# Spreading the softmax maxima over the partitions: 32 by 32 turns and a trip through DRAM in place of TensorE transposes and selector products

## The chip, the cores and the metric

The kernel runs on one core of one Trainium2 chip. The core has five engines that work side by side and meet through semaphores: TensorE (PE in the profile, its weight loads PEld) multiplies matrices into PSUM; VectorE (DVE) and ScalarE (ACT) work element by element; GpSimd (POOL) is used here only to start accumulating transfers; SyncE (SP) starts nearly all other transfers. The transfers themselves run on 16 DMA engines.

The metric is the device time of one execution in microseconds (us); lower is better. The kernel before has a median of 2479.35 us over three runs (2477.35 to 2480.38).

## The reference

One transformer block on x of 4 sequences by 1024 tokens by 512 features, all in float32, conditioned on a vector of 128 numbers per sequence. Cut to what matters:

```python
def norm(x, t, gw, gb, bw, bb):          # RMS norm with gain and bias from the condition t
    g = (t @ gw.T + gb)[:, None, :]
    b = (t @ bw.T + bb)[:, None, :]
    return g * x * rsqrt(mean(x * x) + 1e-6) + b

def attention(x, Wq, Wk, Wv, Wo):        # 16 heads of 32 features
    q, k, v = (x @ W.T for W in (Wq, Wk, Wv))
    attn = einsum('blhd,bmhd->bhlm', q, k) / sqrt(32)
    p = softmax(attn, axis=-1)           # exp(attn - max) / sum of exp
    return einsum('bhlm,bmhd->blhd', p, v) @ Wo.T

h = x + attention(norm(x, ...), ...)
h = h + (silu(n @ gate_w.T) * (n @ hid_w.T)) @ out_w.T      # n = norm(h, ...), hidden width 2048
out = x + h
```

The change concerns the softmax: the maximum over all 1024 keys, for each query and head, has to be subtracted from the scores before the exponential, and the exponentials have to be summed over the keys.

## The kernel before

**Tiling.** Scores are held transposed: the 128 partitions are keys, the free axis is queries. So the maximum over keys, and the sum over keys, run across partitions. One *unit* (number `r`) is 256 keys (`k` = 0, 1: two tiles of 128) for a group of 4 heads (`HG`) and 256 queries (`HQ`): a tile `raw[r]` of 128 partitions by 2 x 4 x 256. Four units (`UN`) cover the 1024 keys and make one *softmax group*, `j = r // UN`. There are 64 groups and 256 units.

**The slots.** A hand-written loop (`while g < END`) emits the instructions of one slot per `g`; `kind = g % 4`. PE, DVE, ACT and POOL run their instructions in exactly the order in which the loop emits them; the order on SP's queue is left to the framework's scheduler. In slot `g` the loop emits

- for unit `g`: `scores` (PE, into the 4-bank PSUM tile with tag `sc`, of which there is one), `keep` (ACT copies it to `raw`), `running_max` (DVE, once per key tile, into `rmax[j]`);
- for unit `g - 5`: `shifted` (DVE subtracts the maxima, spread to all partitions in the tile `shift[j]`, from `raw`) and `exponential` (ACT);
- for unit `g - 6`: `weighted` (PE, product with V into `av`) and `accumulate` (POOL starts a 1 MB accumulating transfer that adds `raw` into the group's first `raw` tile).

So the running maximum of group `j` is complete at the end of a slot of kind 3; `max_T` and `parts` turn and reduce it in the following slot of kind 0; and in the slot of kind 1 after that its first unit is shifted.

**From running maximum to `shift` (before).** `max_T`: PE transposes `rmax` in 8 blocks of 128 by 128 into the `sc` PSUM tile. `parts`: DVE takes the maximum of each row, and splits it by four small instructions into three bfloat16 parts (so that their sum is exact in float32). In kind 1, `parts_T`: PE transposes the parts, ACT copies them to `mT`. `spread`: PE multiplies a 0/1 matrix `select` with `mT`, which writes the negated maxima to all partitions, for two heads at a time; ACT copies each half to `shift`. `shifted` runs in two halves in kind 1, one for each half of the heads.

**Sums.** `fold_sum` (DVE, kind 0) adds the two key-tile halves of the accumulated exponentials of group `g // 4 - 3`, `sums` (PE) multiplies them with a matrix of ones, `sums_out` (ACT) takes the result out, `inverse` (DVE reciprocal) and `normalize` follow, as a rule in kind 2.

**The feed-forward part** runs in the same slots from slot 60 (`FS`) on, one hidden block `p` of 128 features per two slots. It multiplies by Strassen-like sums: seven products, each of two 128-row halves, named by their number: `pair_26` and `copy_156` in the even slot, then the *filler* (`contract`, four output-projection products of 512 columns, evicted by `take_contract`), then `pair_7` and `sub_5` at the end of the even slot; `pair_3`, `gate_tanh`, `pair_15` (of block `p + 1`), `take_5`, `add_15`, `gate`, `pair_4`, `hidden` in the odd slot. `pair_4` adds into a bank half that `sub_5` (DVE) has written, so it waits for `sub_5`. Before slot 60 the PE time is filled by *chains* (projections to keys, queries and values): one per slot, and a second one at the end of even slots. After every eighth group four chains of `project_out` come between.

**Queues.** Weight loads (`load_f`: `fa`, `fw`; `load_ow`: `ow`), keys, queries, V and small round trips through DRAM (`compact`, `take`, `put`, `spread_inverse` for the norms) are all issued by SP.

Of the kernel before, what the change touches and what calls it, by code (L numbers as in the profile page):

```python
# [11 lines left out]
BF16 = mybir.dt.bfloat16  # L12
# [12 lines left out]
def tile_cond_transformer_block(  # L25
# [41 lines left out]
    ident_bf = const.tile([P, P], BF16, tag="ident_bf", name="ident_bf")  # L67
    make_identity(nc, ident_bf)
# [6 lines left out]

    NP = 3 * HG
    split = [const.tile([P, QT, P], BF16, tag=f"split{i}", name=f"split{i}") for i in range(2)]
    for t in split:
        nc.vector.memset(t, 0.0)

    pick = const.tile([NP, HG], F32, tag="pick", name="pick")
    nc.vector.tensor_reduce(pick, ident[:NP, :NP].rearrange("p (h i) -> p h i", i=3), AX.X, ALU.add)
    select = const.tile([NP, HG, P], BF16, tag="select", name="select")
    nc.vector.tensor_copy(select, pick.unsqueeze(2).to_broadcast([NP, HG, P]))
# [26 lines left out]
    raw, rmax, shift, mT, av, acc, avs, oT = {}, {}, {}, {}, {}, {}, {}, {}  # L111
# [215 lines left out]
    def max_T(j: int):  # L327
        pt = ps_sc.tile([P, HQ // P, HG, P], F32, tag="sc", name=f"mt{j}")
        for qt in range(HQ // P):
            for i in range(HG):  # L330
                nc.tensor.transpose(pt[:, qt, i, :], rmax[j][:, i, qt * P : (qt + 1) * P], ident)
        state["mt", j] = pt

    def parts(j: int):

        top = sb.tile([P, HQ // P, HG], F32, tag="top", name=f"top{j}")
        nc.vector.tensor_reduce(top, state.pop(("mt", j)), AX.X, ALU.max)
        to = split[j % 2][:, :, :NP].rearrange("p a (h i) -> p a h i", i=3)
        nc.vector.tensor_scalar_mul(to[:, :, :, 0], top, -1.0)
        nc.vector.tensor_tensor(top, top, to[:, :, :, 0], ALU.add)  # L340
        nc.vector.tensor_scalar_mul(to[:, :, :, 1], top, -1.0)
        nc.vector.scalar_tensor_tensor(to[:, :, :, 2], top, -1.0, to[:, :, :, 1], ALU.mult, ALU.subtract)

    def parts_T(j: int):
        pt = ps.tile([P, HQ // P, P], BF16, tag="w", name=f"pt{j}")
        for qt in range(HQ // P):
            nc.tensor.transpose(pt[:, qt, :], split[j % 2][:, qt, :], ident_bf)
# [350 lines left out]
    with tc.manual_schedule(  # L698
# [69 lines left out]
        while g < END:  # L768
# [14 lines left out]
            if kind == 1 and m_on:  # L783
                parts_T(j_m)
# [219 lines left out]
```

## Time and profile before

| quantity | value |
|---|---|
| median of three runs | 2479.35 us |
| the profiled execution | 2480.0 us, of which the span is 2478.1 us |
| granted TensorE clock, mean | 0.998 |
| first slots (chains beside attention) | 86 to 538 us, 31.3 to 32.9 us per group |
| attention beside the feed-forward part | 538 to 2180 us |
| feed-forward part alone | from 2180 us to the end |
| transfers | 501.69 MB |

A group's period can be read from the two `pt` transposes that occur once per group (line 347). From group 18 on they repeat in a pattern of eight: 43.8 us for the group with the four `project_out` chains, 31.6, 32.0, 31.7, 32.4 us for the four with norm work, and three times 30.55 us with neither. I call the last kind a *plain* period.

How to read the lines: a group row gives line, engine, operation, tiles, shapes and count, then busy us and mean ns of one, then the idle time of the engine just before these instructions and what ended it. A timeline row gives start and length in us, then engine, line, operation and count. For matrix products the length includes the pipeline's run-out, so the distance from one start to the next is what counts. A transfer row gives the issuing queue, count, KB each and the median us from issue to landing.

### The profile page before, as it was taken

What the parts mean: (1) busy time and instruction counts of PE and PEld (TensorE: products, weight loads), DVE (VectorE), ACT (ScalarE), POOL (GpSimd) and SP (SyncE); (2) the same over time, 40 slices, a digit from 0 to 9 for tenths busy, and PEclk for the clock granted to TensorE, in tenths of its full rate; (3) what the DMA queues carried; (4) which work ended last, traced back from release to release, by engine and by line L of the source; (5) the groups of instructions that cost most, each with busy time, mean ns of one, the idle gap of its engine ahead of it and who ended that gap; (6) DMA issues with size and microseconds to landing.
All of it is one profiled execution on the core that took longest, in us unless ns stands there. A gap on an engine that the chain in (4) does not pass through costs nothing. (4 is left out here: it accounts for less than half of the span.)

```text
span 2478.1 us, 71138 instructions
## 1 busy us (share of the span) xinstructions
PE 2396.0 (97%) x31785; PEld 1121.8 (45%) x31785; DVE 1943.7 (78%) x2180; ACT 1412.4 (57%) x1495; POOL 172.4 (7%) x207
## 2 busy tenths in 40 slices
PE   8999999999999999999999999999999999999999
PEld 3333333344444444444444444444444444444444
DVE  2688888888789988998899978997899889843332
ACT  3677777766566656665666656665666566512111
POOL 0000000000000000000000000000000000000000
PEclk9999999999999999999999999999999999999999
DMA  6599998989878888888888888788788888853432
GB/s 214 178 299 251 265 259 221 238 201 238 197 193 203 203 218 200 200 211 214 207 197 207 226 191 204 199 226 203 196 201 212 210 197 199 201 159 116 138 134 71
DMA packets 185982, 501.69 MB, mean 202 GB/s; under 512 B 21319, under 2 KB 78663, under 8 KB 158286
## 3 DMA queue, kind: packets, MB, share of 16 engines
q0 software_dynamic: 28656, 208.68, 43.6%
q1 hardware_dynamic: 156734, 288.47, 34.2%
q8 instruction: 250, 4.10, 0.6%
q14 instruction: 54, 0.44, 0.1%
q10 hardware_dynamic: 288, 0.01, 0.0%
HBM read 246.44 MB, written 41.97 MB: 116 GB/s over the span
## 5 line engine op out<-in xcount | busy, mean ns | idle before, releaser
L363 DVE TENSOR_TENSOR raw<-raw,shift 128x2048 f32<-128x2048 f32 (+1 forms) x320 | 593.9, 1859 | 65.2 <-ACT shift L358 62.3
L366 ACT ACTIVATE raw<-raw 128x2048 f32<-128x2048 f32 x256 | 490.8, 1917 | 214.3 <-DVE raw L363 213.8
L317 ACT COPY raw<-sc 128x2048 f32<-128x2048 f32 x256 | 479.6, 1873 | 169.9 <-PE sc L310 129.7
L322 DVE TENSOR_TENSOR rmax<-rmax,raw 128x1024 f32<-128x1024 f32 x384 | 469.5, 1223 | 53.9 <-ACT raw L317 48.2
L106 PE MATMUL pc<-h,ow 128*32 128x512 f32 x4096 | 467.7, 593 | 2.1 <-DMA ow<-in_out_w 1.1
L376 PE MATMUL av<-raw,v 128*32 128x256 f32 x4096 | 274.9, 386 | 50.0 <-ACT raw L366 50.0
L390 POOL DMA_DIRECT2D raw<-raw x192 | 165.3, 861 | 1991.5 <-ACT raw L366 939.1
L310 PE MATMUL sc<-q,k 32*128 32x256 f32 x4096 | 293.3, 400 | 0.2 <-ACT raw L317 0.2
L106 PE MATMUL pa<-x,fa 128*32 128x256 f32 x4096 | 270.0, 381 | 8.8 <-DVE pa L524 8.5
L106 PE MATMUL pa<-sums,fw 128*32 128x256 f32 x4096 | 267.9, 379 | 0.0
L106 PEld LDWEIGHTS pc<-h,ow 128*32 128x32 f32 x4096 | 128.2, 110 | 245.5 <-issue 226.7
L310 PEld LDWEIGHTS sc<-q,k 32*128 32x128 f32 x4096 | 184.9, 184 | 116.5 <-issue 81.5
L106 PE MATMUL pkq<-y,wkq 128*32 128x512 f32 (+1 forms) x1664 | 231.3, 594 | 4.2 <-ACT y L196 4.1
L376 PEld LDWEIGHTS av<-raw,v 128*32 128x32 f32 x4096 | 107.2, 109 | 175.8 <-ACT raw L366 88.0
L106 PEld LDWEIGHTS pa<-x,fa 128*32 128x32 f32 x4096 | 127.6, 110 | 124.7 <-DVE pa L524 30.5
L106 PEld LDWEIGHTS pa<-sums,fw 128*32 128x32 f32 x4096 | 133.2, 110 | 88.2 <-issue 0.5
L539 ACT COPY pb<-pa 128x256 f32<-128x256 f32 x128 | 46.2, 361 | 181.4 <-PE pa L106 180.3
L577 DVE SCALAR_TENSOR_TENSOR res<-pc,res 128x512 f32<-128x512 f32 x128 | 88.2, 689 | 67.2 <-PE pc L106 62.9
L556 ACT ACTIVATE t<-pa 128x512 f32<-128x512 f32 x128 | 78.1, 610 | 109.9 <-PE pa L106 109.5
L106 PE MATMUL pa<-x,fw 128*32 128x256 f32 x2048 | 135.2, 381 | 0.0
L106 PE MATMUL pb<-x,fw 128*32 128x256 f32 x2048 | 134.0, 379 | 1.2 <-ACT pb L539 1.2
L106 PE MATMUL pb<-sums,fa 128*32 128x256 f32 x2048 | 133.9, 379 | 0.0
(106 smaller groups left out, 2152.4 us busy)
## 6 DMA issues: line engine op xcount, KB each, us to landing
raw<-raw POOLq DMA_DIRECT2D x192, 1024.0 KB, 9.1
fw<-sw SPq DMA_DIRECT2D x128, 512.0 KB, 7.0
fa<-in_gh_w SPq DMA_DIRECT2D x128, 384.0 KB, 5.9
ow<-in_out_w SPq DMA_DIRECT2D x128, 256.0 KB, 2.9
wkq<-in_kq_w SPq DMA_DIRECT2D x32, 512.0 KB, 5.9
v<-vs SPq DMA_DIRECT2D x128, 128.0 KB, 5.0
k<-kqs SPq DMA_DIRECT2D x124, 128.0 KB, 7.0
kqs<-st SPq DMA_DIRECT2D x61, 256.0 KB, 7.7
```

The lines of the kernel that those rows point to most:

```text
L106: nc.tensor.matmul(dst[k : k + n, :], w[:, k : k + n], moving, start=start, stop=stop, skip_group_check=seeded)
L310: nc.tensor.matmul(sc[:, i, k, :], keys[rows, k * P : (k + 1) * P], queries[rows, :], start=True, stop=True)
L317: nc.scalar.copy(raw[r].rearrange("p k h q -> p h k q"), state.pop(("sc", r)))
L322: nc.vector.tensor_tensor(rmax[j], rmax[j], raw[r][:, k, :, :], ALU.max)
L363: nc.vector.tensor_tensor(t, t, s.unsqueeze(1).to_broadcast(list(t.shape)), ALU.add)
L366: nc.scalar.activation(raw[r], raw[r], AF.Exp)
L376: nc.tensor.matmul(av[j][i * DH : (i + 1) * DH, :], v[m, u][:, k, i * DH : (i + 1) * DH], raw[r][:, k, i, :], start=(kt == 0), stop=(kt == ...
L390: nc.gpsimd.dma_start(out=acc[j].rearrange("p k h q -> p (k h q)"), in_=raw[r].rearrange("p k h q -> p (k h q)"), accum_op=ALU.add,)
L539: nc.scalar.copy(bank_b[p][:, RIGHT], bank_a[p][:, RIGHT])
L556: nc.scalar.activation(state["t", p], bank_a[p], AF.Tanh, scale=0.5)
L577: nc.vector.scalar_tensor_tensor(r, pp, 0.5, r, ALU.mult, ALU.add)
```

## The change

- `max_T`, `parts`, `parts_T` and the old `spread` go, and with them the bfloat16 identity, `split`, `pick`, `select`, `mT`.
- `max_blocks` (DVE, at the start of kind 0, ahead of `shifted`): `rmax`, 128 by 1024, is turned within blocks of 32 by 32 by two VectorE transposes of 512 columns, and each result is reduced to 16 columns by a maximum; so each partition then holds the maxima over a quarter of the keys.
- `max_T` (PE, kind 0, after the sums): one matrix product with the identity turns the 128 by 32 result to 32 by 128; DVE takes the maximum over the four quarters (`top`, 32 by 32); SP writes it to DRAM (4 KB).
- `spread` (SP): one transfer reads the 1024 maxima from DRAM and writes them to all 128 partitions (`shift`, 512 KB).
- `shifted` subtracts in one instruction in every slot, kind 1 too, where it stands as in the other slots ahead of the slot's other DVE work.
- `fold_sum` goes; `sums` multiplies both halves on PE (8 products instead of 4), and its result and `max_T`'s go to the `sc` PSUM tile (`spare`) instead of a bank of tag `w`.
- `pair_7` and `sub_5` move from the end of the even slot to the odd slot, ahead of `pair_3`.
- `inverse` moves from the end of kind 2 to the end of kind 0.

```diff
-    def max_T(j: int):
-        pt = ps_sc.tile([P, HQ // P, HG, P], F32, tag="sc", name=f"mt{j}")
-        for qt in range(HQ // P):
-            for i in range(HG):
-                nc.tensor.transpose(pt[:, qt, i, :], rmax[j][:, i, qt * P : (qt + 1) * P], ident)
-        state["mt", j] = pt
-    def parts(j: int):
...
-    def parts_T(j: int):
...
-    def spread(j: int, k: int):
...
-    def shifted(r: int, heads: slice = slice(0, HG)):
...
+    CHUNKS = HG * HQ // 32
+
+    def max_blocks(j: int):
+        state["blocks", j] = sb.tile([P, CHUNKS], F32, tag="blocks", name=f"blocks{j}")
+        half = CHUNKS // 2
         for i in range(2):
+            turned = sb.tile([P, half, 32], F32, tag="t", name=f"turned{j}_{i}", bufs=2)
+            nc.vector.transpose(
+                turned.rearrange("p b c -> p (b c)"),
+                rmax[j][:, i * HG // 2 : (i + 1) * HG // 2, :].rearrange("p h q -> p (h q)"),
+            )
+            nc.vector.tensor_reduce(state["blocks", j][:, i * half : (i + 1) * half], turned, AX.X, ALU.max)
+
+    def spare(g: int):
+
+        return ps_sc.tile([P, HG, 2, HQ], F32, tag="sc", name=f"spare{g}")
+
+    def max_T(j: int, banks):
+        pt = banks[:CHUNKS, 1, 0, :P]
+        nc.tensor.matmul(pt, state.pop(("blocks", j)), ident, start=True, stop=True)
+        top = sb.tile([CHUNKS, 32], F32, tag="top", name=f"top{j}")
+        nc.vector.tensor_reduce(top, pt.rearrange("b (a q) -> b q a", a=P // 32), AX.X, ALU.max)
+        state["top", j] = tc.dram_tile([CHUNKS, 32], F32, name=f"tops{j}")
+        nc.sync.dma_start(out=state["top", j], in_=top)
+
+    def spread(j: int):
+
+        shift[j] = sb.tile([P, HG, HQ], F32, tag="shift", name=f"shift{j}")
+        src = state.pop(("top", j)).rearrange("(o b) q -> o (b q)", o=1)
+        nc.sync.dma_start(
+            out=shift[j].rearrange("p h q -> p (h q)"), in_=src.to_broadcast([P, HG * HQ])
+        )
+
+    def shifted(r: int):
+        s = shift[r // UN].unsqueeze(1).to_broadcast(list(raw[r].shape))
+        nc.vector.tensor_tensor(raw[r], raw[r], s, ALU.subtract)
...
-    def fold_sum(j: int):
-        t = acc[j]
-        nc.vector.tensor_tensor(t[:, 0, :, :], t[:, 0, :, :], t[:, 1, :, :], ALU.add)
...
-    def sums(j: int):
-        total = ps.tile([P, HQ], F32, tag="w", name=f"sum{j}")
+    def sums(j: int, banks):
+        total = banks[:, 0, 0, :]
         a = acc.pop(j)
-        for i in range(HG):
-            nc.tensor.matmul(total[i * DH : (i + 1) * DH, :], ones_sum, a[:, 0, i, :], start=True, stop=True)
+        for k in range(2):
+            for i in range(HG):
+                nc.tensor.matmul(
+                    total[i * DH : (i + 1) * DH, :], ones_sum, a[:, k, i, :], start=(k == 0), stop=(k == 1)
+                )
...
-            if kind == 1 and m_on:
-                parts_T(j_m)
             if g < NR:
                 scores(g)
-            if kind == 1 and m_on:
-                spread(j_m, 0)
-            if kind == 0 and n_on:
-                fold_sum(j_n)
+            if kind == 0 and m_on:
+                max_blocks(j_m)
...
-            if x_on and kind != 1:
+            if x_on:
                 shifted(r_x)
...
-            if kind == 1 and m_on:
-                spread(j_m, 2)
-                mT.pop(j_m)
-                shifted(r_x, slice(0, HG // 2))
-                shifted(r_x, slice(HG // 2, HG))
...
+            if kind == 0 and (m_on or n_on):
+                banks = spare(g)
...
                 evict = chain(g, FG)
-                if kind == 0:
-                    take_sums(j_n)
+                if kind == 0 and n_on:
+                    take_sums(j_n, banks)
+                if kind == 0 and m_on:
+                    max_T(j_m, banks)
+                    spread(j_m)
...
-                if kind == 0 and m_on:
-                    columns[0] = P
-                    max_T(j_m)
-                    parts(j_m)
...
                 copy_156(p)
-                if kind == 0:
-                    take_sums(j_n)
+                if kind == 0 and n_on:
+                    take_sums(j_n, banks)
+                if kind == 0 and m_on:
+                    max_T(j_m, banks)
                 if x_on:
                     exponential(r_x)
-                if kind == 0 and m_on:
-                    max_T(j_m)
-                    parts(j_m)
                 one, two, evict = filler(p)
...
                 if evict is not None:
                     evict()
-                pair_7(p)
-                sub_5(p)
+                if kind == 0 and m_on:
+                    spread(j_m)
...
                     evict = chain(g)
+                pair_7(p)
+                sub_5(p)
                 pair_3(p)
...
-            if kind == 0 and n_on and j_n < direct and j_n % GB == GB - 1:
+            if kind == 0 and n_on and j_n < direct:
                 inverse(j_n)
-                normalize(j_n)
+                if j_n % GB == GB - 1:
+                    normalize(j_n)
             if kind == 2 and n_on and j_n < direct and j_n % GB != GB - 1:
 
-                inverse(j_n)
                 if j_n != GB:
                     normalize(j_n)
```

## The prediction

> **What bounds the kernel now.** I read the page's busy line first. TensorE is busy 97% of the span; no other engine comes near, but VectorE has 78%, and the DMA row shows 80 to 90% for as long as attention runs.
>
> ```profile
> PE 2396.0 (97%) x31785; PEld 1121.8 (45%) x31785; DVE 1943.7 (78%) x2180; ACT 1412.4 (57%) x1495; POOL 172.4 (7%) x207
> ...
> DMA  6599998989878888888888888788788888853432
> ```
>
> Then the groups, shapes kept apart, for what the change removes:
>
> ```profile
> L337 DVE TENSOR_REDUCE top<-mt 128x8 f32<-128x1024 f32 x64 | 78.2, 1221 | 4.5 <-PE mt L331 4.5
> ...
> L331 PE MATMUL mt<-ident,rmax 128*128 128x128 f32 x512 | 69.9, 280 | 0.0
> ...
> L357 PE MATMUL sp<-mT,select 12*128 12x256 bf16 x256 | 49.0, 270 | 1.1 <-ACT shift L358 0.7 <-ACT mT L349 0.4
> ```
>
> Then the timeline of one plain period (two `pt` 30.55 us apart), here TensorE alone at its end, in the slot of kind 0:
>
> ```profile
> 1414.45 0.64 PE L408 MATMUL sum<-raw,ones_sum 128*32 128x256 f32 x8
> 1415.02 1.09 PE L331 MATMUL mt<-ident,rmax 128*128 128x128 f32 x8
> 1416.04 3.64 PE L106 MATMUL pc<-h,ow 128*32 128x512 f32 x32
> 1419.50 1.05 PE L106 MATMUL pb<-x,fw 128*32 128x256 f32 x16
> 1420.49 0.27 PE L347 MATMUL pt<-ident_bf,split 128*128 128x128 bf16 x2
> ```
>
> The reader is to see that PE goes from one start to the next without a hole: the way of the maxima costs PE time, but nobody waits for it, because `contract` (3.45 us) and `pair_7` (1.0 us) run while VectorE makes the parts. VectorE itself is busy 27.6 of the 30.5 us, in an order written out by hand.
>
> Last the transfers, and one round trip through DRAM that is there already (the norms'):
>
> ```profile
> raw<-raw POOLq DMA_DIRECT2D x192, 1024.0 KB, 9.1
> fw<-sw SPq DMA_DIRECT2D x128, 512.0 KB, 7.0
> ...
> ow<-in_out_w SPq DMA_DIRECT2D x128, 256.0 KB, 2.9
> wkq<-in_kq_w SPq DMA_DIRECT2D x32, 512.0 KB, 5.9
> ```
>
> ```profile
> 1208.91 0.24 SPq L156 DMA_DIRECT2D sumsf<-totf  x1
> ...
> 1211.73 0.32 SPq L162 DMA_DIRECT2D fewf<-sumsf  x1
> ```
>
> A 2 KB write was followed by its reader 2.8 us later (1.9 us where `invsf` was followed by `totf`). A 512 KB load lands after 5.9 to 7.0 us while attention runs; in the last stretch, with attention over, the same `fw` load needs 3.1 us:
>
> ```profile
> fw<-sw SPq DMA_DIRECT2D x23, 512.0 KB, 3.1
> ```
>
> **What PE saves.** By distances between starts in the plain period: `pt` 0.20, the two `sp` 0.31 and 0.32, `mt` 1.02: 1.85 us per group go. Added: four more sum products, 0.5 us (the eight records of `sum` take 0.57; bounds 0.44, half of a 16-record product at 0.87, and 0.57), and one product with the identity, 0.27 us (bounds 0.13, one `mt` transpose, and 0.31, one `sp`). Net 1.08 us per group, 69 us over 64. Two waits in kind 0 (`weighted` for the exponential 0.3 us, `pair_26` for `add_15` 0.2 us) may go too: 0.5 us per group.
>
> **What ACT and VectorE save.** ACT loses `mT` 0.36 and two copies of 0.59: 1.54 us per group, worth nothing in itself, as ACT is idle 43% of the time; its cover is that idle time. VectorE loses `fold_sum` 1.22 (64 in 78.0 us), the reduction 1.22, four parts 0.71 and 0.2 from halving `shifted` (2.49 against 2.28): 3.35 us. It gains two block turns, two reductions of 512 columns and a small maximum of 128 columns. No turn is in this trace. The nearest rows are 128x512 operations at 0.69; the ends are 0.43 (a 128x256 row, were it twice as fast) and 1.22 (a 128x1024 row, were it half as fast). I take 0.69 and for the small one 0.28 (between 0.17 for 8 columns and 0.43 for 256): 3.04 us, or 2.5 to 4.1. Busy time hardly changes; the place does.
>
> **What it waits for.** Before, `shift` came from PE and ACT within kind 1. Now it needs a write to DRAM, its completion, and a 512 KB read to all partitions, and `shifted` of kind 1 stands in VectorE's order before `sub_5`. Behind a late `shifted` wait `sub_5`, both maxima, `add_15`, `gate` and `hidden`; `pair_4` on PE waits for `sub_5`, and all PE work behind `pair_4` with it. Moving `pair_7` and `sub_5` into the odd slot makes this link: before, `sub_5` stood ahead of `shifted`. On SP, `fa`, `fw`, key and V loads queue behind the two waits (some 2.4 us each period); three `fw` buffers and five key and five V buffers cover that, and without them PE would wait as long.
>
> **The period, walked.** S is the end of the first `shifted` of a group, T the start of the next kind 0 (its `scores`). PE after S: `sub_5` 0.4, `pair_4` 0.98, `scores` 1.08, `weighted` 0.88, `pair_26` 1.73, `contract` 3.43, then kind 3: 1.08 + 0.88 + `pair_7` 0.87 + `pair_3` 0.87 + `pair_15` 1.72 + `pair_4` 0.98. So T = S + 14.9. VectorE's kind 3 ends at T + 1.4, since `add_15` waits for ACT's `take_5` behind the exponential. `max_blocks` 2.6 (starts follow each other 0.07 us faster than durations say) to T + 4.0; `shifted` 2.2 to T + 6.2, `top` to T + 6.5. PE meanwhile: 1.08 + 0.88 + 1.73 + sums 1.0 = T + 4.7, `max_T` to T + 5.0, `contract` to T + 8.4. Write issued T + 6.6, read 2.4 us later (middle of 1.9 and 2.8) at T + 9.0, landing after L, `shifted` 2.4 with its wake-up: next S = T + 11.4 + L. In the gap VectorE has `running_max`, `take_contract` and the reciprocal that was moved there, until T + 11.0. A period is 26.3 + L, where before it is 30.55. **The break-even is L = 4.2 us.**
>
> L is the disputed price. Nearest rows: 5.9 (`wkq`, 512 KB) and 7.0 (`fw`, 512 KB from DRAM scratch), both under traffic; quiet, 3.1. The read meets an accumulating transfer (three per group at 9.1 us fill 27 of 30.5 us) and comes 0.5 us after an `ow` load on its own queue, so it is nearer to the loaded rows: I take 6.4, ends 3.1 and 8.8 (`fw` between 1000 and 1400 us).
>
> Beside this row stands a rule. The Trainium skill, "DMA: Bandwidth & Descriptors", section "Anatomy of one DMA", gives each transfer about 2.0 us fixed plus its bytes at 436 GB/s, mostly the receipt of the write. By it the 512 KB take 3.2 us, as in the quiet rows here, but not the 7.0 us of the loaded ones; the period would be 29.5 us and the kernel faster by some 60 us. The same section says the receipt is longest where the target is DRAM, which speaks against putting the maxima there; 1.9 to 2.8 us here.
>
> **The sum.** After slot 60 there are 50 groups. 44 have no `project_out`: 26.3 + 6.4 - 30.55 = +2.15 us each, +95. Six have four chains of 3.4 us, one of them before `pair_4` of kind 1, which covers the wait: -1.1 each, -7. The first 14 groups have no `pair_4`, only `weighted` of kind 2 behind its exponential: kind 0 takes 1.1 + 0.9 + 3.45 + 1.0 + 0.3; `top` at T + 7.0, read T + 9.5, with 5.8 (`wkq` there) landed 15.3, `shifted` 17.6, exponential 19.6, where PE wanted it at 16.6; then 0.9 + 6.9 + 1.1 + 0.9 + 3.45 gives 32.8 against a mean of 32.3 before: +7. Together +95; the profiled execution's 2480.0 becomes 2575, and as it stands 0.65 us above the median, 2574 to compare with 2479.35. 0.2% (5 us) is what a measurement can tell.
>
> **The rivals.**
> (1) The trip is hidden or short. For it: the quiet 3.1 us, and the reciprocal put into the gap. Against it: DMA at 84% there. At L = 3.1 the plain period is 29.4 (-51), the long ones -7, the first part PE-bound at some 30.1 (-31): 2391. It decides from L below 4.2.
> (2) SP holds the write or the read behind a blocked load: `ow` is seen waiting for the end of `contract`, T + 8.4. A write put behind it is 2.1 us later, 64 times: 2574 + 134 = 2708. For it: SP's order is not written in the kernel. Against it: the loop emits the write first.
> (3) The wait and PE's saving cancel, L between 4.0 and 5.2: 2470 to 2520. For it: a read issued after the accumulate has nearly ended. Against it: all loaded 512 KB rows.
>
> **How the numbers follow.** My case, L from 5.2 to 8.8: 0.56. Rival 1: 0.22, rival 2: 0.10, rival 3: 0.12, of it 0.03 within 0.2%, 0.02 below and 0.07 above. Faster 0.24, same 0.03, slower 0.73. For my case alone the range is 2520 to 2660 (turns at 0.43 or 1.22 move it by -33 or +68). Reaching to rival 1's middle and into rival 2, 2440 to 2680 leaves 0.1 out on either side.
>
> **What would show it.** `shifted` with an idle time ended by the DMA of `shift`, some 4 us per group; PE idle before `pair_4` in kind 1, ended by `sub_5`; landing of `shift` at 6 to 7 us; plain periods of 32 to 33.5 us; `max_blocks` rows at 0.69; the tail after attention unchanged. Wrong if `shift` lands in under 4.2 us, or if a turn costs much more than 0.69.

## The result and the profile after

The changed kernel takes 2912.53 us (median of four runs, 2898.77 to 2919.92) where the kernel before takes 2479.34 us: a ratio of 1.174 with an interval of 1.173 to 1.176. That is 433 us more. The prediction had the sign and the waiting instruction right and the size wrong: it foresaw 95 us more.

The page of the changed kernel, from a run of 2911.5 us (busy line, the rows of PE, its granted clock and the DMA share over the span, the costliest groups, the transfers):

```profile
span 2909.7 us, 71319 instructions
...
PE 2449.3 (84%) x31866; PEld 1157.2 (40%) x31866; DVE 1908.1 (66%) x2048; ACT 1330.1 (46%) x1303; POOL 172.4 (6%) x205
...
PE   8778778888788888887988878887888788889999
...
PEclk9899889999899989998999989999999899999999
DMA  5697788877777777777767767777677777773442
...
L351 DVE TENSOR_TENSOR raw<-raw,shift 128x2048 f32<-128x2048 f32 x256 | 584.9, 2285 | 418.4 <-DMA shift<-tops 418.4
...
L93 PE MATMUL pb<-sums,fa 128*32 128x256 f32 x2048 | 170.0, 459 | 271.4 <-DVE pb L531 271.4
L364 PE MATMUL av<-raw,v 128*32 128x256 f32 x4096 | 304.6, 420 | 101.6 <-ACT raw L354 101.4
...
raw<-raw POOLq DMA_DIRECT2D x192, 1024.0 KB, 9.3
fw<-sw SPq DMA_DIRECT2D x128, 512.0 KB, 7.4
...
shift<-tops SPq DMA_DIRECT2D x64, 512.0 KB, 5.1
```

TensorE falls from 97% to 84% of the span. VectorE's instructions have grown no costlier (1908 us busy against 1944), but 418 us of idle time stand in front of `shifted` (line 351), and the transfer of `shift` ended all of it. The next two rows show how that reaches TensorE: 271 us in front of `pair_4` (`pb<-sums,fa`), ended by VectorE's `sub_5` (line 531), which stands behind `shifted`; and 101 us in front of `weighted`, ended by the exponential, mostly in the first part of the kernel, where there is no `pair_4`. The mean granted clock fell from 0.998 to 0.924, and TensorE's busy time rose by 53 us although the change takes work from it. That second effect is not in the prediction.

The waits of SyncE in the changed kernel (line waited for: us in total, times, longest us):

```profile
SPq L345 <- DMA tops<-top: 282.4, 64, 9.1
SPq L339 <- DVE top L337: 241.2, 46, 6.9
...
SPq L416 <- DMA out<-res: 43.1, 6, 8.8
```

The read (line 345) waits 282 us for the completion of the 4 KB write, 4.4 us each time. The time from one issue to the other is longer: after the first part it is 4.7 us in the mean of 45 groups, and 8.3 us in six others, each the one just ahead of a group with `project_out` chains. Line 416 loads the residual, and its waits come back where those six groups are explained.

One plain period (start, length, engine, line, operation; the idle time before it, and what ended it, in brackets):

```profile
1601.89 0.32 SPq L345 DMA_DIRECT2D shift<-tops  x1
...
1603.05 1.05 PE L93 MATMUL pa<-sums,fw 128*32 128x256 f32 x16
...
1606.78 2.29 DVE L351 TENSOR_TENSOR raw<-raw,shift 128x2048 f32<-128x2048 f32 x1 [5.24 <-DMA shift<-tops]
1608.99 0.42 DVE L531 TENSOR_TENSOR pb<-pb,p 128x256 f32<-128x256 f32 x1
...
1609.47 1.94 PE L93 MATMUL pb<-sums,fa 128*32 128x256 f32 x16 [5.38 <-DVE pb L531]
...
1611.34 2.09 PE L297 MATMUL sc<-q,k 32*128 32x256 f32 x16
...
1626.84 1.15 PE L297 MATMUL sc<-q,k 32*128 32x256 f32 x16
...
1632.06 0.30 PE L335 MATMUL spare<-ident,blocks 128*32 128x128 f32 x1 [0.49 <-ACT total L400]
...
1632.89 0.27 DVE L337 TENSOR_REDUCE top<-spare 32x32 f32<-32x128 f32 x1
1633.19 0.32 SPq L339 DMA_DIRECT2D tops<-top  x1
...
1638.27 0.33 SPq L345 DMA_DIRECT2D shift<-tops  x1
```

This is the prediction's walk, in the measured times of one period. S, the end of `shifted`, is 1609.07, and T, the start of `scores` of the next kind 0, is 1626.84. The write leaves at T + 6.35, the read 5.08 us behind it. At the top of the same list a read at 1601.89 lets `shifted` start 4.89 us later. The sum 17.8 + 6.35 + 5.08 + 4.89 + 2.29 is 36.4 us, and the two reads stand 36.4 us apart. Plain periods differ in their parts: over the twelve groups that were plain before and don't stand just ahead of `project_out` chains, S to T is 17.2 us in the mean, write to read 4.7, and the read's issue to the start of `shifted` 5.5. Look at the lengths of the products too: after the idle time 16 records take 1.94 and 2.09 us, at the next kind 0 the same `scores` take 1.15.

The same kernel in windows around that wait (start and end, us, busy of PE, PEld, DVE, ACT, POOL, then the granted clock, the DMA share and GB/s) shows why:

```profile
1604.00:1608.00 4.00, 0.09 (x4) 0.00 (x0) 1.22 (x1) 0.00 (x0) 0.00 (x0) 1.00 0.97 230
1608.00:1609.40 1.40, 0.00 (x0) 0.00 (x0) 1.40 (x3) 0.29 (x1) 0.00 (x0) 0.67 1.03 233
1609.40:1611.30 1.90, 1.83 (x16) 0.60 (x16) 1.87 (x3) 1.90 (x3) 0.00 (x0) 0.50 1.04 233
...
1613.30:1615.00 1.70, 1.70 (x20) 0.79 (x20) 1.70 (x2) 1.47 (x1) 0.00 (x0) 0.50 1.00 387
1615.00:1617.00 2.00, 2.00 (x40) 1.13 (x36) 1.97 (x3) 0.40 (x1) 0.00 (x0) 0.93 0.20 65
```

TensorE stops at 1604.1. The means of the windows put the fall of the clock to one half at about 1608.5, 4.4 us later, and its return at about 1615.3, 5.8 us after the restart. The Trainium skill, "TensorE: Matmul & The Clock Gate", Part 1, "The HAM clock gate", describes such a gate: the clock halves after at least one idle window of about 3.4 us, and returns after at least one busy window of about 3.4 us. The halving is as the page says; the two times in this example are longer, which "at least one" allows.

Where the 433 us lie can be read from the distances between groups, sorted by the place of the group. "Long" groups have the four `project_out` chains, the "group before" is the one just ahead of them, which has a 1 MB load of the residual on its way. Mean period in us:

```
                      13 first   6 long   6 group before   38 other   sum of the 63
before                  32.24     43.82       30.55          31.52       2063.2
after                   41.49     50.01       43.96          36.51       2490.5
difference, summed      +120      +37         +80            +190        +427
no trip                 32.89     44.50       29.13          29.56       1992.5
previous maxima         34.95     44.72       39.77          31.59       2161.6
busy wait               41.71     49.81       47.27          35.35       2468.1
P7 even                 41.90     47.62       43.84          36.25       2470.8
no accumulate           34.75     44.59       30.45          30.38       2056.5
write from ScalarE      40.09     49.97       40.24          36.66       2455.5
```

(The lower rows are the experiments below.) The tail is as it was: from the turn of the last group's maxima (`pt` before, `max_T` after) to the end are 329 us before and 339 after, and the second holds that group's trip.

### The profile page after: what moved, and what is told of

It is laid out like the page before. It is cut to its first block, busy times and chain, and to the rows that moved or that the text cites. A ratio compares the mean times of both kernels' runs of the same rounds, so it can differ in the third digit from the quotient of the medians.

```text
span 2909.7 us, 71319 instructions
## 1 busy us (share of the span) xinstructions
PE 2449.3 (84%) x31866; PEld 1157.2 (40%) x31866; DVE 1908.1 (66%) x2048; ACT 1330.1 (46%) x1303; POOL 172.4 (6%) x205
## 3 DMA queue, kind: packets, MB, share of 16 engines
q1 hardware_dynamic: 169022, 322.29, 33.5%
## 5 line engine op out<-in xcount | busy, mean ns | idle before, releaser
L351 DVE TENSOR_TENSOR raw<-raw,shift 128x2048 f32<-128x2048 f32 x256 | 584.9, 2285 | 418.4 <-DMA shift<-tops 418.4
L93 PE MATMUL pc<-h,ow 128*32 128x512 f32 x4096 | 477.1, 594 | 0.5 <-DMA ow<-in_out_w 0.5
L93 PE MATMUL pb<-sums,fa 128*32 128x256 f32 x2048 | 170.0, 459 | 271.4 <-DVE pb L531 271.4
L364 PE MATMUL av<-raw,v 128*32 128x256 f32 x4096 | 304.6, 420 | 101.6 <-ACT raw L354 101.4
L297 PE MATMUL sc<-q,k 32*128 32x256 f32 x4096 | 330.5, 442 | 0.1
L297 PEld LDWEIGHTS sc<-q,k 32*128 32x128 f32 x4096 | 206.1, 206 | 205.6 <-issue 127.1
L93 PE MATMUL pkq<-y,wkq 128*32 128x512 f32 (+1 forms) x1976 | 248.0, 623 | 4.1 <-ACT y L183 4.1
L93 PEld LDWEIGHTS pc<-h,ow 128*32 128x32 f32 x4096 | 165.3, 110 | 208.7 <-issue 137.5
L93 PEld LDWEIGHTS pb<-sums,fa 128*32 128x32 f32 x2048 | 69.0, 124 | 346.4 <-DVE pb L531 300.7
L93 PE MATMUL po<-oT,wo 128*32 128x512 f32 x1024 | 127.8, 643 | 14.8 <-DVE h L546 11.7
```

The source lines that it names most:

```text
L93: nc.tensor.matmul(dst[k : k + n, :], w[:, k : k + n], moving, start=start, stop=stop, skip_group_check=seeded)
L297: nc.tensor.matmul(sc[:, i, k, :], keys[rows, k * P : (k + 1) * P], queries[rows, :], start=True, stop=True)
L351: nc.vector.tensor_tensor(raw[r], raw[r], s, ALU.subtract)
L364: nc.tensor.matmul(av[j][i * DH : (i + 1) * DH, :], v[m, u][:, k, i * DH : (i + 1) * DH], raw[r][:, k, i, :], start=(kt == 0), stop=(kt == ...
```

## The experiments

The theory after the result (A): the round trip, write, completion, read to all partitions, stands alone in the path from one group to the next, and it is longer than foreseen because the write completes late while an accumulating transfer of 1 MB is on its way. The rivals: the trip's traffic slows everything else (B); the halved clock makes most of the loss by itself (C); the move of `pair_7` and `sub_5` makes the link (D). The expectations use the letters C and D, with or without a number, for the rival of their own run; outside them, the letters are the ones of this list. Unless a line says otherwise, each time is from one run beside a run of the kernel before on the same chip, which took 2478.5 to 2478.9 us.

**The read takes the previous group's maxima.** The write and the read are both still made, 64 times, but the read no longer waits for this group's write and is issued before it.

```diff
-        src = state.pop(("top", j)).rearrange("(o b) q -> o (b q)", o=1)
+        src = state.pop(("top", j - 1)) if j else state["top", j]
+        src = src.rearrange("(o b) q -> o (b q)", o=1)
...
+                if kind == 0 and m_on:
+                    spread(j_m)
                 if kind == 0 and n_on:
                     take_sums(j_n, banks)
                 if kind == 0 and m_on:
...
-                if kind == 0 and m_on:
-                    spread(j_m)
```

> The changed kernel, but the read that fills shift takes the maxima of the group before, which lie in DRAM long since, and is issued ahead of this group's write. All work and both transfers stay; only the wait for the write's completion goes (softmax does not change with what is subtracted; group 0 alone still reads its own). Theory A (the time is the latency of write and read, standing between the first shifted and pair_4, and the halved TensorE clock after the idle time): read issued at T + 6.3 instead of T + 11.4, first shifted ends at T + 13.8, about when PE comes to pair_4; no long idle, no halved clock; plain periods 29 to 30.5 us, 2380 to 2470 us. Rival B (the added traffic of 34 MB slows everything else): traffic is the same, still above 2800 us. Rival C (the wait counts, the clock does not): 2912 less 64 x 5 us, some 2590 us.

2579.35 us: 333 of the 433 us are gone, with the same bytes on the way. So rival B falls. It is over 100 us more than the expectation gave theory A, and near the 2590 us of the rival that counts the wait and not the clock; but it doesn't speak for that rival, since `shifted` still waits 152 us for `shift` here, and the granted clock is 0.973. The transfers and the wait of this kernel:

```profile
shift<-tops SPq DMA_DIRECT2D x64, 512.0 KB, 7.2
```

```profile
DVE raw L352 <- DMA shift<-tops: 152.0, 55, 9.7
```

Issued earlier, in the middle of an accumulating transfer, the read needs 7.2 us instead of 5.1. What the write's completion cost was thus in part a shift in time: in the changed kernel the read leaves 8.2 us (median) after the last accumulate was started, when that transfer has nearly ended, and here 3.9 us after.

**No trip at all.** Neither write nor read; `shift` is a tile of zeros set once.

```diff
-        state["top", j] = tc.dram_tile([CHUNKS, 32], F32, name=f"tops{j}")
-        nc.sync.dma_start(out=state["top", j], in_=top)
...
+        if "zero" not in state:
+            state["zero"] = sb.tile([P, HG, HQ], F32, tag="shift", name="shift")
+            nc.vector.memset(state["zero"], 0.0)
+        shift[j] = state["zero"]
```

> The changed kernel without the write and the read: shift is one tile of zeros, set once (the turned and reduced maxima are still made, and not used; softmax does not change with what is subtracted, and these scores are far from overflow). It asks what the rest of the change is worth when nobody waits. Theory A: PE saves 1.1 us per group and some waits, less what the moved pair_7 and the sums cost by themselves (29 and 20 us in the kernel before): 2390 to 2450 us, clock 0.998, plain periods about 29 us. Rival C2 (spare bank, moved pair_7 and doubled sums eat the saving): 2470 us and more.

2405.48 us, 73 us below the kernel before; a plain period is 29.0 us. So what TensorE saves is real, and in sum near the 69 us of the prediction; the trip costs 2912.5 - 2405.5 = 507 us. TensorE's 31,866 instructions are busy 2311.2 us here, at a granted clock of 0.996, and 2449.3 us in the changed kernel, at 0.924. The same instructions take 138 us more, and the lower clock is what differs; even counted in full, that is under a third of the 433 us.

**Work in the wait.** To see what the clock costs in time, idle products with the identity keep TensorE busy while it waits: 18 in kind 1 ahead of `pair_4`, where no other chain stands there, and 28 ahead of the first `weighted` of a group before slot 60.

```diff
+    def idle(dst, n: int):
+        for _ in range(n):
+            nc.tensor.matmul(dst, ones_mean, ident, start=True, stop=True)
...
+            if r + UN + 2 < FS:
+                idle(av[j][:, :P], 28)
...
+                if kind == 1 and x_on and not extra:
+                    idle(spare(g)[:, 0, 0, :P], 18)
                 pair_4(p)
```

> The changed kernel, with products that nothing reads put where PE waits: 18 of 128 by 128 by 128 ahead of pair_4 in kind 1 without a chain (about 4.9 us at full clock), 28 ahead of the first weighted product of a group in kind 2 before slot 60. The wait itself stays. Theory A: granted clock stays at 1.0 through the wait, pair_4 and the two stages after it take 0.98, 1.08 and 0.9 instead of 1.9, 2.0 and 1.7 us; 2.5 to 2.9 us less in each of some 50 groups, 2740 to 2800 us. Rival C (the slow products after the wait come from something else, waits for PSUM or transfers): they stay slow and the time stays at 2900 us or rises.

2888.21 us, only 24 us less (the four runs of the changed kernel spread over 21): a miss. The clock rises to 0.970, and behind the wait of a plain period the products run at their full pace (`pair_4` 1.07 us, `scores` 1.15). S to T shrinks there from 17.2 us in the mean to 15.0 in nearly every one, which is the prediction's 14.9. A plain period goes from 36.4 to 34.3. The first part does not move (41.71 against 41.49 us). The group before the long one gets 3.3 us longer, and all of that stands in the trip: from `top` to the start of `shifted` it takes 21.3 us instead of 18.0. The idle products do not cause it directly, since the 4.3 us that they take fit into a wait of over 11 us. So the halved clock is a real cost, about 2 us in a plain period, but it is not the main one. Rival C falls, although the clock was not restored everywhere.

**`pair_7` and `sub_5` back in the even slot.**

```diff
                 if evict is not None:
                     evict()
+                pair_7(p)
+                sub_5(p)
...
-                pair_7(p)
-                sub_5(p)
                 pair_3(p)
```

> The changed kernel with pair_7 and sub_5 back at the end of the even slot; all else as changed. Theory A: pair_4 no longer waits, but the weighted product of kind 2 waits for the exponential behind the same shifted, some 2 us later in PE's order; PE comes there by 0.87 us earlier, for want of pair_7. The gain is 0 to 1.5 us per group after slot 60: 2830 to 2920 us. Rival D (the move of pair_7 made the link that costs, as the prediction put it): the wait falls off by most of its length, 2550 to 2700 us.

2889.87 us, as theory A had it. The wait does not go, it changes its place. The wait of TensorE that was in front of `pair_4` now stands in front of `weighted`:

```profile
PE av L364 <- ACT raw L354: 317.2, 54, 14.6
```

Rival D falls: the link over `sub_5` is the place where the trip shows first, and the softmax itself is the next.

**The move alone, in the kernel before.** The same two calls moved in the old kernel, and nothing else.

```diff
-                pair_7(p)
-                sub_5(p)
...
                 if kind == 3 and extra:
                     evict = chain(g)
+                pair_7(p)
+                sub_5(p)
                 pair_3(p)
```

> The kernel before with one part of the change alone: pair_7 and sub_5 in the odd slot. shift still comes from PE and ACT. Theory A: the link from shifted over sub_5 to pair_4 is there, but shifted ends 2 us before PE comes to pair_4, and the parts are ready 1 us before pt even without pair_7 ahead of it: 2470 to 2495 us. Rival D (the move itself costs): 2530 us and more.

2508.15 us, 29 us more than before, and more than the foreseen bound. A plain period gets 0.5 us longer; the six long groups go from 43.8 to 46.1. The prediction priced this move by itself at nothing.

**The sums alone, in the kernel before.** `fold_sum` taken out, 8 products instead of 4.

```diff
-            nc.tensor.matmul(total[i * DH : (i + 1) * DH, :], ones_sum, a[:, 0, i, :], start=True, stop=True)
+        for k in range(2):
+            for i in range(HG):
+                nc.tensor.matmul(
+                    total[i * DH : (i + 1) * DH, :], ones_sum, a[:, k, i, :], start=(k == 0), stop=(k == 1)
+                )
...
-            if kind == 0 and n_on:
-                fold_sum(j_n)
```

> The kernel before with one part of the change alone: the sums of both halves on PE, without fold_sum. Theory A: PE gains 0.5 us of work in each group and is the bound, VectorE loses 1.2 us that nobody waited for, apart from 0.2 to 0.5 us of waits in kind 0: 2480 to 2515 us.

2499.21 us, 20 us more: 0.4 us in a plain period, 0.3 us in the mean of all, where the prediction's sum had 0.5. TensorE is full, and VectorE's saved 1.2 us buys nothing.

**The accumulating transfers left out.** This tells why the write takes 5 us: because of what is on the way beside it, or because of its shape (32 rows of 128 bytes).

```diff
         if u == 0:
             acc[j] = raw[r]
-        else:
+        elif False:
             nc.gpsimd.dma_start(
```

> The changed kernel without the accumulating transfers (the sums then hold only the first unit of each group; this part of the result is left out). It asks why the 4 KB write takes 5.1 us to complete. Theory A1 (its packets stand among those of the 1 MB accumulating transfer that was started 4.7 us before): write lands in 2 to 2.8 us, the read in 3.5 to 4.5, first shifted ends at T + 15 to 16, little idle time is left, 2450 to 2560 us. Rival A2 (the write is slow for its shape, 32 rows of 128 bytes): still 5 us, total not under 2700 us.

2470.28 us. That is below the kernel before, but the two do not do the same work, since here 192 transfers of 1 MB are left out. The transfers of this kernel:

```profile
shift<-tops SPq DMA_DIRECT2D x64, 512.0 KB, 3.7
...
tops<-top SPq DMA_DIRECT2D x64, 4.0 KB, 2.1
```

The write lands after 2.1 us instead of 5.2, the read after 3.7 instead of 5.1. The shape is not the cause. The prediction's 2.4 us for the write and its lower end of 3.1 us for the read are about the prices of this quiet state.

**The write from ScalarE's queue.** Is the write late behind other work in SyncE's queue?

```diff
-        nc.sync.dma_start(out=state["top", j], in_=top)
+        nc.scalar.dma_start(out=state["top", j], in_=top)
```

> The changed kernel with the 4 KB write issued by ACT instead of SP, so on another queue; the read stays on SP. It asks whether the write's 5 us are spent behind SP's own earlier loads or on DMA engines that the accumulating transfer keeps busy. Theory A1 (engines shared with the accumulate): the time from write to read stays at 4.5 to 5.5 us, total 2880 to 2940 us. Rival A3 (first come, first served on SP's queue): it falls to 2 to 2.8 us, total 2650 to 2760 us.

2873.37 us, 39 us less and a little below the expected range. The transfer row of this kernel:

```profile
tops<-top ACTq DMA_DIRECT2D x64, 4.0 KB, 5.0
```

From a queue without other traffic the write lands as late. So it does not wait in its queue; with the run before this one, what it waits for is the accumulating transfer that runs beside it. The trace of the changed kernel fits: in the example above the accumulate was started at 1628.49; the DMA share is 1.04 from 1634 to 1636 and 0.10 from 1636 to 1638, and the read leaves at 1638.27. The write completes some 2 us after the big transfer has drained. The Trainium skill, "DMA: Bandwidth & Descriptors", section "Queues, rings and completion order", says that an engine takes its queues in turn, a packet at a time. By that alone a 4 KB write would wait for a packet or two, not for the whole transfer. The same section also says that the signal of a completion lands only after every earlier write of that engine, across its queues, which would fit a write that ends with the accumulate. No run here separates the two, so the mechanism stays open.

The 39 us show something else. In the six groups before a long one SyncE is behind with its own transfers: the load of the residual (line 416) stands in its order and waits, those behind it pile up, and the write leaves 3.0 to 4.3 us after `top` is ready (0.03 us in a plain group). From ScalarE's queue it leaves at once there, and these groups take 40.2 us instead of 44.0, 22 us less in sum. The 13 first groups take 18 us less, and the rest a little more.

**The trip one slot earlier.** The maxima are taken over the first three units of the group, at the start of kind 3, so that the whole slot lies between the read and its use.

```diff
+            early = kind == UN - 1 and g < NR
-            if kind == 0 and m_on:
-                max_blocks(j_m)
+            if early:
+                max_blocks(g // UN)
...
+                if early:
+                    max_T(g // UN, banks)
                 if kind == 0 and m_on:
-                    max_T(j_m, banks)
                     spread(j_m)
```

> The changed kernel with the trip one slot earlier: the maxima are taken over the first three units of a group (768 of 1024 keys; softmax does not change with what is subtracted, as long as the last quarter's scores do not exceed that maximum by some 88, where the exponential would overflow), turned in kind 3, written at its end, and read in kind 0. The two running_max of the last unit go too. Theory A: write issued some 0.5 us before T, read issued at T + 4.8, landed by T + 10 to T + 12.5 (5 to 7.5 us, amid the accumulate), shifted ends at T + 12.4 to 14.9, against T + 13.6 when PE comes to pair_4: wait of 0 to 1.7 us, no halved clock, 2370 to 2460 us. Rival C2 (the added products and the spare bank on PE cost as much as the transposes saved): 2480 us and more even with no wait for shift.

2660.33 us: a miss, by 200 us. The write lands after 4.1 us, but the read falls into the next accumulate, 6.9 us in the median, and `shifted` starts on average 8.1 us after the read was issued. Of the 166 us that `shifted` waits for `shift`, half fall on the six groups before a long one, 11.6 to 15.7 us in each, where the read leaves 9 to 13 us behind the write; in most plain groups it waits under 2 us. And `scores` of the following slot uses the same PSUM tile as `max_T`, so TensorE waits there for the small maximum, 64 us in all. One slot, some 8 us, is not enough cover where the trip is long: from `top` to its use it takes 14 us in the mean.

**Two slots earlier.** The maxima over the first two units, at kind 2; the read is issued in kind 3; two `shift` tiles, so that the read does not wait for the last use of the old one (paid for by one V tile less).

```diff
-        shift[j] = sb.tile([P, HG, HQ], F32, tag="shift", name=f"shift{j}")
+        shift[j] = sb.tile([P, HG, HQ], F32, tag="shift", name=f"shift{j}", bufs=2)
...
+            early = kind == 2 and g < NR
-            if kind == 0 and m_on:
-                max_blocks(j_m)
+            if early:
+                max_blocks(g // UN)
...
+                if early:
+                    max_T(g // UN, banks)
+                if kind == 3 and g < NR:
+                    spread(g // UN)
```

> The changed kernel with the trip two slots earlier: the maxima are taken over the first two units of a group (512 of 1024 keys), turned and written in kind 2, read in kind 3 into the second of two shift buffers (the V buffers go from five to four to make room); running_max of the other two units goes. The result is the same as long as no score of the other half exceeds that maximum by some 88. Theory A: the trip of some 5 + 7 us and SP's queueing fit into the 20 us between kind 2 and kind 1 of the next group, shifted waits in few groups or none, no halved clock: 2390 to 2460 us, some 30 us above the kernel without the trip at most. Rival B (traffic of 34 MB slows the rest): 2480 us and more with no wait for shift.

2468.74 us (2465.28 to 2470.26), ratio 0.996 with an interval of 0.994 to 0.997; slightly above what was expected. The same trip, the same traffic (`shift` still lands after 5.4 us), and 444 us less than the changed kernel. The two waits that matter now:

```profile
PE spare L335 <- DVE blocks L327: 87.2, 47, 4.5
...
DVE raw L351 <- DMA shift<-tops: 11.7, 5, 4.4
```

The wait for `shift` is gone (11.7 us, before the first groups have settled). In its place TensorE waits for the reductions of `max_blocks`, because `max_T` stands ahead of `contract` in PE's order.

**The same with `pair_7` in the even slot.** Since the move cost 29 us alone, undoing it should have paid here.

```diff
                 if evict is not None:
                     evict()
+                pair_7(p)
+                sub_5(p)
...
-                pair_7(p)
-                sub_5(p)
                 pair_3(p)
```

> As the kernel with the trip two slots earlier, and pair_7 and sub_5 back at the end of the even slot. Theory A: with no wait for shift left, the move of pair_7 costs what it cost in the kernel before, 29 us: 2365 to 2435 us, 10 to 30 us less than with pair_7 in the odd slot. Rival D2 (here it gives nothing, since no parts are waited for): equal within 10 us.

2490.38 us (2485.87 to 2492.79), ratio 1.005 with an interval of 1.003 to 1.007: 22 us slower than with the move, the wrong sign. With the early trip the move is worth having; the price of the move in the old order does not carry over to the new one. Why is left open.

**`max_T` between the two halves of `contract`.** One call moved, so that 1.9 us of products that wait for nothing stand ahead of it.

```diff
-                if early:
-                    max_T(g // UN, banks)
                 if x_on:
                     exponential(r_x)
                 one, two, evict = filler(p)
                 one()
+                if early:
+                    max_T(g // UN, banks)
                 two()
```

> The kernel with the trip two slots earlier (maxima over the first two units), with max_T after slot 60 between the two halves of contract instead of ahead of them, so that PE multiplies while VectorE still makes the blocks. Theory A: of the 87 us that PE waited there for the blocks some 50 to 70 us go, part of it comes back as a wait of scores for the reduction of the result: 2405 to 2440 us, below both kernels. Rival E (the wait only moves to scores, which need the same bank): 2455 to 2475 us.

2421.80 us (2419.24 to 2425.24), ratio 0.9775 with an interval of 0.976 to 0.979: as expected, and faster than both kernels. The waits of this kernel:

```profile
PE spare L335 <- DVE blocks L327: 13.7, 23, 1.7
...
DVE raw L351 <- DMA shift<-tops: 11.3, 4, 5.2
```

and its transfers:

```profile
shift<-tops SPq DMA_DIRECT2D x64, 512.0 KB, 8.4
...
tops<-top SPq DMA_DIRECT2D x64, 4.0 KB, 3.8
```

The read lands after 8.4 us, slower than in any other kernel here, and nobody waits for it: the length of the trip no longer matters once two slots lie over it. Part of the relief is work that is no longer done: the maxima over the other half of the keys were four instructions on VectorE per group, whose busy time falls from 1908 to 1612 us. The kernel without a trip took all maxima and was 16 us faster still, so that relief is not what the time hangs on once the trip is covered; what it is worth by itself was not run. The version costs a freedom: the shift is the maximum over 512 of the 1024 keys. The softmax is the same for every shift as long as no exponential overflows, so it holds while the scores of the other keys exceed that maximum by less than about 88.

## Why the prediction was right and wrong

**The direction and the link held.** `shifted` idles for `shift`, `sub_5` stands behind it, `pair_4` and all PE work behind `sub_5`: 418 and 271 us in the first profile. Of the signs that the prediction named, these waits, the 0.69 us of the `max_blocks` rows and the tail came as foreseen; the plain periods (36.4 us, not 32 to 33.5) and the landing of `shift` (5.1 us, not 6 to 7) did not.

**What TensorE saves held, in sum.** 69 us foreseen, 73 measured without the trip. As a sum it is partly luck: the 73 us also hold the move of `pair_7`, which costs 29 us by itself in the kernel before and was priced at nothing, and the waits that the prediction left out of its 69. They are spread otherwise, too: the 38 other groups save 1.96 us each, and the 13 first lose 0.65. The both-half sums cost 0.4 us in a plain period against 0.5. The turn of 128 by 512, which no trace had shown, takes 0.70 us (0.69 taken); the reduction behind it 0.69; the small maximum 0.27 (0.28 taken).

**What failed first is the write's completion**, "read 2.4 us later". Measured: 5.4 us in the first groups, then 4.7 in the mean of 45 groups and 8.3 in the six before a long one. The two rows it came from, the 2 KB writes of the norms, had 1.9 and 2.8 us and were priced as if the moment did not matter. The trace of before holds fourteen such pairs of a write and its reader, from 1.5 to 4.0 us apart. The prediction weighed the accumulating transfer for the 512 KB read, and left it out for the 4 KB write that is issued in its midst. Without the accumulate the write takes 2.1 us, so the rows were right for a quiet moment.

**The read's L was too high, for the same reason.** 6.4 us taken; 5.1 in the median, 4.9 in the period shown. Since the write ends with the accumulate, the read starts behind it, as the third rival had it. In the walk the two errors partly cancel: +2.7 and -1.5. L was called the disputed price, and at 5.1 it lies in the window of the third rival, 2470 to 2520 us, while the time is some 400 us above: L was not what decided. The rule of the Trainium skill that the prediction sets beside this row ("DMA: Bandwidth & Descriptors", section "Anatomy of one DMA") is a fit for transfers that GpSimd starts. This read is started by SyncE; it lands after 3.7 us without the accumulates, against the 3.2 us estimated from that fit.

**The clock is missing in the walk.** "T = S + 14.9" is what it takes at full clock, and the kernel with work in the wait shows 15.0. The changed kernel takes 17.8 in the period shown and 17.2 in the mean of the plain ones, because the clock is halved for what follows the wait. The prediction named a wait of some 4 us per group (`shifted` waits 6.5 us in the mean) and did not ask what it does to the products behind it. Together the three make the period shown: 32.7 foreseen, +2.9 for the clock, +2.7 for the write, -1.5 for the read, -0.4 for the small steps: 36.4. By the means of the plain periods the clock and the write have some 2.3 us each and the read -0.9.

**The groups with more traffic were wrong by more, and they hold most of the miss.** The prediction had -1.1 us for a long group, +2.15 for the one before it and +0.5 for the first groups; measured are +6.2, +13.4 and +9.25. Of the 332 us that are missing between 95 and 427, those 25 groups make some 224 us: 7.3 x 6 + 11.2 x 6 + 8.7 x 13. In the group before the long one, the residual's load of 1 MB and an accumulate are both on the way, and the timeline of the changed kernel there shows `top`, write, read and use as far apart as this:

```profile
1350.51 0.33 SPq L416 DMA_DIRECT2D res<-in_x  x1
...
1354.33 0.27 DVE L337 TENSOR_REDUCE top<-spare 32x32 f32<-32x128 f32 x1
1354.41 1.52 SPq L489 DMA_DIRECT2D fa<-in_gh_w  x1
...
1356.03 0.87 SPq L275 DMA_DIRECT2D k<-kqs  x1
1357.00 0.55 SPq L286 DMA_DIRECT2D v<-vs  x1
...
1357.59 1.03 SPq L339 DMA_DIRECT2D tops<-top  x1
...
1365.68 0.32 SPq L345 DMA_DIRECT2D shift<-tops  x1
...
1371.74 2.29 DVE L351 TENSOR_TENSOR raw<-raw,shift 128x2048 f32<-128x2048 f32 x1 [11.96 <-DMA shift<-tops]
...
1374.43 1.93 PE L93 MATMUL pb<-sums,fa 128*32 128x256 f32 x16 [11.56 <-DVE pb L531]
```

The trip takes 14 us from the write where the plain period has 10, and the write itself leaves 3 us after `top`, because SyncE is still issuing loads that piled up behind the residual's. Over the six groups it is held 3.6 us in the mean, and write to read takes 8.3 us instead of 4.7: these two make 7.2 of the 7.6 us by which the six exceed a plain period of the same kernel. That is the mechanism of the second rival, some loads ahead of the write, in six groups where the rival had it in all 64, and at 3.6 us where it had 2.1; it was given too little place as a part of the likeliest case. In the first groups write to read takes 5.4 us, not 2.5, and the read 8.0 us to its use, not 5.8; that is 5.1 of the 8.7 us, and the rest is open. In the long groups the chain does cover most of the wait of `pair_4`, which is 0 to 2.6 us there, but the next chain behind it then waits 2.3 us in each of the six, in five of them for `gate`, which stands behind the same `shifted`. Of their +6.2 us, the move of `pair_7` alone makes another 2.3 by the run of the kernel before.

**The move of `pair_7` and `sub_5` was priced only as a link.** Alone it costs 29 us in the kernel before, 0.5 in a plain period, which the walk did not have as a term.

**The unknown was too narrow.** The range allowed for one late transfer per group, not for two and a slower engine behind them, and took one price of the write, 2.4 or 2.5 us, for all 64 trips.

## What to carry to other kernels

A dependent trip through DRAM is at least two transfers in a row, and each is to be priced at the moment when it is issued: a small write issued beside a big accumulating transfer took 5 us here, and 2 us without it. Look at what stands ahead of it in its queue too, group by group and not in the commonest group alone. Price the wait itself and what comes behind it: in the period shown, TensorE ran the first 5.8 us behind its idle time at half clock. If the value can be had earlier, move the trip instead of shortening it: two slots of cover took 444 us off with the same bytes (and with some 300 us less work for VectorE), one slot did not suffice, and another 47 us came from putting work that waits for nothing ahead of the one product that waits.

## What the runs showed of the hardware

- A write of 4 KB from SBUF to DRAM completes after 5.2 us (median) with accumulating 1 MB transfers on their way, 2.1 us without them, and it is nearly the same from another engine's queue (5.0 us).
- A read of 4 KB from DRAM spread to 128 partitions (512 KB written) lands after 3.7 us without accumulating transfers, after 5.1 us where most are issued some 8 us behind the start of one, and after 5.4 to 8.4 us in four kernels that issue most of them sooner behind it.
- In the wait shown, TensorE's granted clock halved some 4.4 us after its last product and was full again some 5.8 us after the restart. Over the kernel this made 138 us of busy time, but only some 2 us of a plain period of 36.4.
- VectorE turned 128 by 512 float32 in 32 by 32 blocks in 0.70 us, nearly the same as a reduction of that size (0.69).
